# A graph network with routed experts: attention queries in two fp32r parts, expert lists cleared on SyncE's queue

## The chip, the cores and the metric

The kernel runs on one core of one Trainium2 chip. The core has five engines that run side by side, each with its own instruction stream: TensorE (PE, matrix products into PSUM; its weight loads are shown apart as PEld), VectorE (DVE), ScalarE (ACT), GpSimd (POOL) and SyncE (SP). SyncE, ScalarE and GpSimd also issue transfers between SBUF and the device's memory, which 16 DMA engines carry out; "SPq" and "ACTq" in a profile are the issuing instructions on SyncE and ScalarE. Engines wait for each other through semaphores.

The metric is the device time of one execution in microseconds (us). Before the change it is 3965.03 us, the median of three runs (3961.12, 3965.03, 3967.85).

## The reference, cut to what matters

`x` is 3125 nodes by 256 features, with a graph of 53,125 edges (`src`, `dst`, sorted by `dst`). Four pairs of layers follow; each adds to `x`, and each starts with a layer normalization:

```python
x = x + _L0_gnn_ref(_layernorm(x), edge_attr_8, Wq, Wk, Wv, Wo, src, dst)  # attention over the edges, 8 heads
x = x + _L0_ffn_ref(...)   # shared MLP and 4 small experts, the top 2 by a gate
x = x + _L1_gnn_ref(...)   # three rounds of mean aggregation over the edges
x = x + _L1_ffn_ref(...)   # 8 large experts, each node goes to its top 2
x = x + _L2_gnn_ref(...); x = x + _L2_ffn_ref(...)
x = x + _L3_gnn_ref(...); x = x + _L3_ffn_ref(...)
```

The attention:

```python
q = (nfeat @ Wq.T).reshape(n, HEADS, HEAD_DIM) / SCALING
k = (nfeat @ Wk.T).reshape(n, HEADS, HEAD_DIM)
v = (nfeat @ Wv.T).reshape(n, HEADS, HEAD_DIM)
attn = jnp.einsum('ehd,ehd->eh', k[src], q[dst]) + attn_bias
m = jax.ops.segment_max(attn, dst, num_segments=n)
a = jnp.exp(attn - m[dst])
a = a / jax.ops.segment_sum(a, dst, num_segments=n)[dst]
out = jax.ops.segment_sum(v[src] * a[:, :, None], dst, num_segments=n)
return out.reshape(n, FEAT) @ Wo.T
```

## The kernel before, in words

The 3125 nodes are 25 tiles (T) of 125 rows (P), kept in SBUF as `x` for the whole kernel.

**Attention** (`attention`, from L1529). Keys and values of all nodes are written to `kv_d` in the device's memory. Then one loop over the 25 tiles of destination nodes. A tile has a window of 18 chunks (WC) of 128 edges, in three groups of 6 (PC). For a tile:

- `one_hot` makes a one-hot matrix `oh` of each chunk's 128 edges against the tile's 125 rows (bf16), on VectorE.
- `one_hot_turned` transposes it chunk by chunk on TensorE (L1721); ScalarE copies it to `oht` (L1722), 125 by 18 by 128, bf16.
- `queries` multiplies the normalized rows with `Wq`. ScalarE scales the result to `q` (L1710). `q` is then cut into three bf16 parts whose sum is the fp32 value: VectorE rounds the first (L1711) and subtracts it (L1712), ScalarE rounds the second (L1713), VectorE subtracts again for the third (L1714). They lie in `q_t`.
- `logits` has GpSimd gather each edge's key and value row (L1559, one indirect transfer per chunk into a `kv` buffer for 6 chunks; 7 such buffers). For each chunk TensorE multiplies `oht` with the three parts of `q_t`, adding up in PSUM (L1735, 54 products a tile, each with its own weight load); that brings each edge the query of its destination. VectorE multiplies with the keys (L1738) and reduces by head (L1739).
- `sums_of` adds the edges' bias (L1745), takes a first exp (L1748) and sums it per destination with `oh` (L1751, L1753).
- `weights_of` turns the exponent of that sum into a shift `m` (L1759, bf16), brings it to the edges with `oht` (L1763, 18 products of 8 columns), subtracts (L1764), and takes the final exp (L1768).
- `weighted` multiplies values by weights (L1773) and adds them up per destination with an fp32 copy of `oh` (L1778, L1780, `acc`). When `acc` has read a `kv` buffer, GpSimd may gather into it again.
- `normed`, `normed_turned`, `projected` divide, transpose and multiply with `Wo`, and add to `x` (L1804).

The loop is staggered: tile t's logits run beside the weights and sums of tile t-1 and the one-hots and queries of tile t+1.

**Blocks** (`blocks`, from L1855) turn the edge lists into two dense tables of edge counts, `at_d` and `an_d`, that the later convolutions read. For each of 25 steps t: one-hots on VectorE, products (L1954, L1956) into `ab`, a store of `ab` to `at_d`, 25 transposes (L1966) into `an`, a store of `an` to `an_d`. Both stores are on SyncE's queue, each as two transfers (`move`, L105 and L106). `ab` and `an` have two buffers each. The steps are generated one by one between the products of `experts0`, the first experts' layer, so both share the engines.

**Convolutions** (`convolutions`, from L2074) make three passes over `an_d` (`block_pass`, products L2055). Per pass there are seven groups of tiles, and `post` finishes each.

**Expert lists.** For the 8 large experts each node's row is scattered into `xs_d`, a list of 26,880 rows of 260 floats (27.96 MB). Rows that no node fills must be zero, so the list is cleared first. `clear_slots` (L246) is a generator: it makes a tile `nothing` of zeros, 128 by 260, and at each step issues one transfer on ScalarE's queue for one expert (L252, 3380 KB in packets of 1040 B), and a last small one for the spare block (L258). `convolutions` creates it (L2103) and asks for a step at the end of each `post` of the first two passes (L2141). The transfers are collected in `xs_fill`. The router's scatters (L1000, about 2174 to 2373 us) wait for all of them.

Nothing in the code writes the order out by hand: the framework that builds the kernel plans each engine's order by estimated times and due dependencies. A call that is made later in the code can stand earlier on its engine. The profile shows where things came to lie.

Of the kernel before, what the change touches and what calls it, by code (L numbers as in the profile page):

```python
# [68 lines left out]
def gnn_ffn_kernel(ctx: ExitStack, tc: tile.TileContext, a, out: bass.AP):  # L69
# [175 lines left out]

    def clear_slots(pool):  # L246

        nothing = pool.tile([128, DX], F32, name="nothing", bufs=1)
        nc.vector.memset(nothing, 0.0)
        xs_fill.clear()  # L250
        for e in range(8):
            xs_fill.append(nc.scalar.dma_start(  # L252
                xs_d[e * EB * BLK:(e + 1) * EB * BLK, :].rearrange("(p r) d -> p (r d)", p=128)
                .rearrange("p (h d) -> p h d", d=DX),
                nothing.unsqueeze(1).to_broadcast([128, EB * BLK // 128, DX])))
            yield

        xs_fill.append(nc.scalar.dma_start(  # L258
            xs_d[8 * EB * BLK:, :].rearrange("(p r) d -> p r d", p=128),
            nothing.unsqueeze(1).to_broadcast([128, BLK // 128, DX])))  # L260

# [1267 lines left out]
    def attention():  # L1529
# [10 lines left out]
        with ExitStack() as es:  # L1540
# [144 lines left out]

            pool = tiles
            psum = es.enter_context(tc.tile_pool(name="ps_att", bufs=3, space=PSUM, reuse_waits="tile"))

# [15 lines left out]
            def queries(s):  # L1704

                ps = psum.tile([P, D], F32, name="sm")
                product(ps, [(s.lt[:, k, :], wq[:, k, :]) for k in range(2)])
                s.q = pool.tile([P, 3, D], BF16, name="q_t")
                q = pool.tile([P, D], F32, name="q")
                nc.scalar.activation(q, ps, AF.Copy, scale=float(HD) ** 0.5)  # L1710
                nc.vector.tensor_copy(s.q[:, 0, :], q)  # L1711
                nc.vector.tensor_sub(q, q, s.q[:, 0, :])  # L1712
                nc.scalar.copy(s.q[:, 1, :], q)  # L1713
                nc.vector.tensor_sub(s.q[:, 2, :], q, s.q[:, 1, :])  # L1714

            def one_hot_turned(s):
                s.oht = pool.tile([P, WC, 128], BF16, name="oht")
                for c0 in range(0, WC, PC):
# [7 lines left out]
            def logits(s, p):  # L1726
# [4 lines left out]
                for c0 in range(0, PC, 2):  # L1731
                    ps = psum.tile([128, 2, D], F32, name="qx")
                    for c in range(2):
                        for k in range(3):
                            nc.tensor.matmul(ps[:, c, :], s.oht[:, p * PC + c0 + c, :], s.q[:, k, :],  # L1735
                                             start=(k == 0), stop=(k == 2))
                    k_ = kv[:, c0:c0 + 2, KO:VO]
                    nc.vector.tensor_mul(k_, k_, ps)  # L1738
# [16 lines left out]
            def weights_of(s):  # L1755

                m = pool.tile([P, H], BF16, name="m")
                c = 8.0 * math.log(2.0)
# [96 lines left out]
    def blocks(pool, psum):  # L1855
# [84 lines left out]
        ps_n = psum.tile([P, T], F32, name="bdeg", bufs=1)  # L1940

        def hot(name, v, t, n):
            o = pool.tile([128, GT, n], BF16, name=name)
            one_hots(o, v[:, t * GT:(t + 1) * GT, :], iota_h)
            return o

        for t in range(T):
# [14 lines left out]
            for s0 in range(0, T, 8):  # L1962
                n = min(8, T - s0)
                ps = psum.tile([128, 1024], BF16, name="bk")
                for s in range(s0, s0 + n):
# [3 lines left out]
                         ps.rearrange("p (s r) -> p s r", s=8)[:P, :n, :P])  # L1969
            move(nc.sync, an_d[:, t, :], an)  # L1970
            yield
# [21 lines left out]
    def halves(hp, v):  # L1993


        nc.scalar.copy(hp[:, 0], v)  # L1996
        nc.vector.tensor_sub(hp[:, 1], v, hp[:, 0].bitcast(F32))
# [76 lines left out]
    def convolutions(big, bpool):  # L2074
# [7 lines left out]
        with ExitStack() as es:  # L2082
# [19 lines left out]
            pool, route, behind, late = cpool, [], [], []  # L2102
            clear = clear_slots(big)  # L2103

# [5 lines left out]
            for l, bias in enumerate((b0, b1, b2)):  # L2110
                def post(t0, n, agg, l=l, bias=bias):
# [28 lines left out]
                    if l < 2:  # L2140
                        next(clear, None)  # L2141
                        return
# [180 lines left out]
```

## Time and profile before

| | |
|---|---|
| median of three runs | 3965.03 us |
| the profiled execution | 3998.39 us, span 3996.5 us |
| granted TensorE clock, mean | 0.872 |
| busy: PE, PEld, DVE, ACT, POOL | 86%, 64%, 43%, 26%, 15% of the span |
| L1735, 1350 products | 262.0 us busy |
| L1559, 450 gathers | 438.6 us busy, 476.0 us idle before them |
| L252, 8 clears on ScalarE's queue | median 12.05 us each, 1469.8 to 1553.4 us; L258 12.60 us |

How to read it. Times in a row count from the start of the span. "out<-in" names the tile that is written and those that are read; a number in brackets at a row's end is how long the engine was idle before, and what ended that. "issue" means that the profile shows nothing that it waited for. "remote" means that a semaphore moved and the profile does not tell by whom. The granted clock is the share of TensorE's full clock in a stretch; a product at 0.5 takes twice as long. The stages that matter here: attention until about 1060 us, the blocks beside `experts0` until 1447, the rest of `experts0` until 1587, the convolutions from there.

### The profile page before, as it was taken

The page shows a single profiled execution, that of the slowest core. Times are in us where ns is not written, and L with a number is a line of the kernel's source. Part 1 is how long each engine was busy: PE and PEld are TensorE (multiplying, and loading weights), DVE is VectorE, ACT ScalarE, POOL GpSimd, SP SyncE. Part 2 cuts the span into 40 slices and gives each one's busy share as a digit, 9 for nine tenths or more (in the row PEclk, how much of TensorE's full clock was granted, in tenths as well). Part 3 has the DMA queues.
Part 4 walks back from the last instruction along what each step waited for, and adds up shares of the span by engine and source line. Part 5 has one row for each costly group of instructions (what it writes and reads, how often), then busy time and mean ns, then how long its engine had stood idle before and what let it go on. Part 6 is the DMA issues. An engine that isn't in the chain of part 4 may idle for free.

```text
span 3996.5 us, 45148 instructions
## 1 busy us (share of the span) xinstructions
PE 3427.4 (86%) x16645; PEld 2542.0 (64%) x16645; DVE 1728.9 (43%) x4687; ACT 1032.2 (26%) x1931; POOL 609.2 (15%) x588
## 2 busy tenths in 40 slices
PE   6466676676689985999999969997999999999998
PEld 2344555555457652788887848886885555568765
DVE  5355555555667742423235551112562111154562
ACT  1111111211224320333232322222443232332120
POOL 1445444544200000000000132221000000000000
PEclk9677777777767885999999869998989999999898
DMA  6445445444223458334343435665530000024101
GB/s 171 146 135 149 126 124 146 140 129 125 73 80 121 132 162 211 82 97 108 95 110 75 105 115 163 181 185 147 131 88 17 8 16 8 14 63 104 39 1 33
DMA packets 283611, 415.30 MB, mean 104 GB/s; under 512 B 40844, under 2 KB 233137, under 8 KB 283377
## 3 DMA queue, kind: packets, MB, share of 16 engines
q1 hardware_dynamic: 191122, 233.61, 21.1%
q0 software_dynamic: 51568, 134.33, 12.4%
q10 hardware_dynamic: 40687, 44.34, 4.3%
q8 instruction: 135, 2.21, 0.2%
q14 instruction: 99, 0.81, 0.1%
HBM read 313.72 MB, written 98.40 MB: 103 GB/s over the span
## 4 chain that ended last, share of the span: by engine, by line
PE 63%; DVE 2%; ACTq 2%; DMA 1%; ACT 1%; issue 1%; POOL 0%; SPq 0%; DVEq 0%; POOLq 0%
PE po L233 19%; PE agg L2055 18%; PE hid_ps L233 13%; PE tr L233 3%; ACTq L252 1%; PE row L233 1%; PE po L231 1%; PE tok L1439 1%; PE bk L1966 1%; PE tr L223 1%; PE bk L1954 1%; PE tr L2130 1%; DMA x_d<-ys,to 1%; PE bdeg L1956 1%; PE pair L233 0%
## 5 line engine op out<-in xcount | busy, mean ns | idle before, releaser
L2055 PE MATMUL agg<-cnt_f,hp 125*128 125x500 f32 (+1 forms) x3500 | 740.1, 372 | 23.7 <-ACT hp L1996 23.7
L2055 PEld LDWEIGHTS agg<-cnt_f,hp 125*128 125x128 f32 x3500 | 643.9, 191 | 108.6 <-ACT hp L1996 25.0
L1559 POOL DMA_INDIRECT kv<-kv_d,src_w x450 | 438.6, 975 | 476.0 <-PE acc L1780 319.0
L1735 PE MATMUL qx<-q_t,oht 125*128 125x256 bf16 x1350 | 262.0, 355 | 154.2 <-issue 88.7
L2033 ACT CAST cnt_f<-blk 125x500 fp32r<-125x500 bf16 (+1 forms) x435 | 245.9, 566 | 485.5 <-PE agg L2055 468.9
L2033 DVE CAST cnt_f<-blk 125x500 fp32r<-125x500 bf16 (+1 forms) x440 | 185.3, 423 | 295.3 <-PE agg L2055 250.2
L1735 PEld LDWEIGHTS <-oht 125*128 125x128 bf16 x1350 | 164.6, 124 | 230.0 <-issue 180.8
L1286 DVE SCALAR_TENSOR_TENSOR x<-po,gall,x 125x256 f32<-125x256 f32 x200 | 93.8, 483 | 416.2 <-PE po L233 415.7
L1280 ACT ACTIVATE h<-hid_ps,shift,scale 128x500 f32<-128x500 f32 (+1 forms) x224 | 161.9, 723 | 375.9 <-PE hid_ps L233 375.4
L1780 PE MATMUL acc<-kv,oh_f 128*125 128x265 f32 x900 | 212.3, 396 | 21.5 <-DVE kv L1773 21.5
L1738 DVE TENSOR_TENSOR kv<-kv,qx 128x512 f32<-128x512 f32 x225 | 147.3, 682 | 149.5 <-remote 104.6
L1780 PEld LDWEIGHTS acc<-kv,oh_f 128*125 128x125 f32 x900 | 170.1, 191 | 60.8 <-DVE kv L1773 29.0
L233 PE MATMUL hid_ps<-xe,wslot 128*128 128x256 f32 x832 | 194.8, 387 | 10.7 <-DVE xe L1125 10.5
L233 PE MATMUL po<-wslot,h 128*125 128x256 f32 x800 | 203.0, 386 | 0.1
L233 PE MATMUL hid_ps<-h,wslot 128*128 128x500 f32 (+1 forms) x448 | 193.2, 554 | 4.1 <-ACT h L1280 0.6
L233 PEld LDWEIGHTS po<-wslot,h 128*125 128x125 f32 x800 | 145.0, 187 | 75.2 <-ACT h L1280 27.2
L1000 POOL DMA_INDIRECT xs_d<-r_l,pos x50 | 59.5, 1190 | 871.3 <-DVE r_l L996 740.8
L233 PE MATMUL hid_ps<-v_rows,wslot 128*128 128x500 f32 (+1 forms) x448 | 187.2, 538 | 0.0
L233 PE MATMUL po<-wslot,hid 128*128 128x256 f32 x832 | 183.8, 379 | 0.0
L233 PEld LDWEIGHTS hid_ps<-xe,wslot 128*128 128x128 f32 x832 | 148.9, 191 | 44.1 <-DVE xe L1125 13.8
L233 PEld LDWEIGHTS po<-wslot,hid 128*128 128x128 f32 x832 | 158.1, 190 | 21.5
L1132 ACT ACTIVATE hid<-hid_ps,wslot 128x256 f32<-128x256 f32 x208 | 97.0, 474 | 279.8 <-PE hid_ps L233 279.8
(480 smaller groups left out, 4755.6 us busy)
## 6 DMA issues: line engine op xcount, KB each, us to landing
wslot<-in_ex_W SPq DMA_DIRECT2D x52, 1024.0 KB
blk<-an_d SPq DMA_DIRECT2D x60, 546.9 KB
xs_d<-nothing ACTq DMA_DIRECT2D x8, 3380.0 KB
blk<-at_d SPq DMA_DIRECT2D x40, 546.9 KB
blk<-an_d SPq DMA_DIRECT2D x45, 410.2 KB
at_d<-ab SPq DMA_DIRECT2D x25, 683.6 KB
an_d<-an SPq DMA_DIRECT2D x25, 683.6 KB
blk<-at_d SPq DMA_DIRECT2D x30, 410.2 KB
```

The costliest lines, as they stand in the source:

```text
L223: nc.tensor.transpose(ps[:, i * P:(i + 1) * P], src[:, i, k * 128:(k + 1) * 128], ident[:P, :P])
L233: nc.tensor.matmul(ps, l, r, start=(bias is None and i == 0), stop=(i == last))
L1000: st = nc.gpsimd.indirect_dma_start(out=xs_d, in_=l2[:, i, :], in_offset=None, out_offset=bass.IndirectOffsetOnAxis(ap=self.pos[s][:, t0 + ...
L1132: nc.scalar.activation(hid[:, m, :], ps[:, :BLK], AF.Gelu, bias=c[:, 4 + m:5 + m])
L1280: nc.scalar.activation(dst[:, m, :c], ps[:, :c], AF.Relu, bias=shift[:, l, col:col + 1], scale=scale[:, l, col:col + 1])
L1286: nc.vector.scalar_tensor_tensor(x[:, t0 + i, :], po, gating.all[:, t0 + i, e:e + 1], x[:, t0 + i, :], ALU.mult, ALU.add)
L1559: nc.gpsimd.indirect_dma_start(out=kv[:, c, KO:], out_offset=None, in_=kv_d, in_offset=bass.IndirectOffsetOnAxis(ap=src_i[:, at + c:at + c ...
L1735: nc.tensor.matmul(ps[:, c, :], s.oht[:, p * PC + c0 + c, :], s.q[:, k, :], start=(k == 0), stop=(k == 2))
L1738: nc.vector.tensor_mul(k_, k_, ps)
L1780: nc.tensor.matmul(s.acc[:, :D + H + 1], of[:, c, :], kv[:, c, AO:VO], start=(p == 0 and c == 0), stop=(p == 2 and c == PC - 1))
L2033: to(f[:, :n, :], part[0][:, :n, m % MB, :])
L2055: nc.tensor.matmul(ps[f][:, :c], hp[:, m, k, f * 128:(f + 1) * 128], got[:, :c], start=(m == 0 and k == 0), stop=(m == T - 1 and k == 1))
```

## The change

Two things are changed.

In the attention, `q` is cut into two fp32r parts in place of three bf16 ones, by `halves`, a function that the convolutions already use: ScalarE rounds the first part, VectorE subtracts. `oht` becomes fp32r to match and gets a pool of its own, `att_o`, that is opened when the pools of the setup are closed. There are two products per chunk in place of three. `m`, which shares `oht` as weights, becomes fp32r too.

The clearing of `xs_d` is cut into ten transfers of 2.80 MB in place of eight and a small one, with packets of 3120 B from a three times wider tile `nothing`. They are issued on SyncE's queue instead of ScalarE's, in `blocks` after the stores of every second step from t=4 on. Each waits for an earlier `an` store (`stored[-3]`, that of two steps before). The convolutions issue none any more.

```diff
-    def clear_slots(pool):
+    def clear_slots(pool, behind=lambda: None):
-        nothing = pool.tile([128, DX], F32, name="nothing", bufs=1)
+        nothing = pool.tile([128, 3 * DX], F32, name="nothing", bufs=1)
         nc.vector.memset(nothing, 0.0)
+        slots = xs_d.rearrange("(p a r) d -> a p (r d)", p=128, a=10).rearrange("a p (h w) -> a p h w", w=3 * DX)
         xs_fill.clear()
-        for e in range(8):
-            xs_fill.append(nc.scalar.dma_start(
...
+        for part in range(10):
+            st, other = nc.sync.dma_start(slots[part], nothing.unsqueeze(1).to_broadcast([128, 7, 3 * DX])), behind()
+            if other is not None:
+                tc.add_manual_dep(st.ins, other.ins.name, data_dep, reason="in turn")
+            xs_fill.append(st)
             yield
-        xs_fill.append(nc.scalar.dma_start(
-            xs_d[8 * EB * BLK:, :].rearrange("(p r) d -> p r d", p=128),
...
+            turned_pool = es.enter_context(tc.tile_pool(name="att_o", bufs=2, reuse_waits="tile"))
...
-                s.q = pool.tile([P, 3, D], BF16, name="q_t")
+                s.q = pool.tile([P, 2, D], F32R, name="q_t")
                 q = pool.tile([P, D], F32, name="q")
                 nc.scalar.activation(q, ps, AF.Copy, scale=float(HD) ** 0.5)
-                nc.vector.tensor_copy(s.q[:, 0, :], q)
-                nc.vector.tensor_sub(q, q, s.q[:, 0, :])
-                nc.scalar.copy(s.q[:, 1, :], q)
-                nc.vector.tensor_sub(s.q[:, 2, :], q, s.q[:, 1, :])
+                halves(s.q, q)
...
-                s.oht = pool.tile([P, WC, 128], BF16, name="oht")
+                s.oht = turned_pool.tile([P, WC, 128], F32R, name="oht")
...
-                        for k in range(3):
+                        for k in range(2):
                             nc.tensor.matmul(ps[:, c, :], s.oht[:, p * PC + c0 + c, :], s.q[:, k, :],
-                                             start=(k == 0), stop=(k == 2))
+                                             start=(k == 0), stop=(k == 1))
...
-                m = pool.tile([P, H], BF16, name="m")
+                m = pool.tile([P, H], F32R, name="m")
...
+        stored = []
+        clear = clear_slots(pool, lambda: stored[-3])
...
-            move(nc.sync, an_d[:, t, :], an)
+            stored.append(move(nc.sync, an_d[:, t, :], an))
+            if t > 2 and t % 2 == 0:
+                next(clear, None)
             yield
...
-            clear = clear_slots(big)
...
                     if l < 2:
-                        next(clear, None)
                         return
```

`halves`, unchanged:

```python
def halves(hp, v):
    nc.scalar.copy(hp[:, 0], v)
    nc.vector.tensor_sub(hp[:, 1], v, hp[:, 0].bitcast(F32))
```

## The prediction

> **What bounds the kernel now.** I read four views, in this order: the page's chain of waits, that chain in order of time, the timeline of the stages that the diff touches, and rows of single tiles. The chain says TensorE almost throughout, with one part that is no engine's work:
>
> ```profile
> PE 63%; DVE 2%; ACTq 2%; DMA 1%; ACT 1%; issue 1%; POOL 0%; SPq 0%; DVEq 0%; POOLq 0%
> ```
>
> In order of time that part lies in one place, the end of the first experts' layer:
>
> ```profile
> 1481.66 9.27 ACTq L252
> 1491.63 11.71 ACTq L252
> ...
> 1516.76 11.86 ACTq L252
> 1528.88 12.31 ACTq L252
> 1541.81 11.51 ACTq L252
> 1554.41 11.71 issue
> ```
>
> These six make 68.4 us. They are the clears of `xs_d`. ScalarE's timeline shows what they do: the code asks for one per group of the convolution, but all nine were placed ahead of it, between the last activations of `experts0`, and the queue holds the engine while its transfers drain:
>
> ```profile
> 1528.67 0.21 ACT L707 ACTIVATE g<-g 125x12 f32<-125x12 f32 x1 [11.91 <-issue]
> 1528.69 12.50 ACTq L252 DMA_DIRECT2D xs_d<-nothing  x1
> 1541.24 0.57 ACT L750 ACTIVATE s<-tr,wslot 128x375 f32<-128x375 f32 x1 [12.36 <-issue]
> ```
>
> The reader sees activations of 0.2 and 0.6 us waiting 12 us each. The stretches (PE, PEld, DVE, ACT, POOL busy; clock; DMA share; GB/s) say the same: from 1470 to 1570 the DMA engines are full (1.08, 280 GB/s) and TensorE works 53 of 100 us, while in the block building before it DMA is at 0.39:
>
> ```profile
> 160.00:1060.00 900.00, 624.05 (x3808) 469.10 (x3807) 505.01 (x805) 166.06 (x321) 399.50 (x409) 0.75 0.43 125
> 1130.00:1450.00 320.00, 292.95 (x2241) 218.34 (x2240) 218.00 (x390) 108.95 (x177) 0.15 (x1) 0.76 0.39 123
> 1470.00:1570.00 100.00, 53.01 (x127) 25.76 (x126) 14.31 (x47) 7.86 (x16) 0.00 (x0) 0.67 1.08 280
> ```
>
> Attention (160 to 1060) is bound by none of these alone. POOL issues a tile's 18 gathers (1.25 us apart, 22.6 us), then waits for `acc` of the tile before to free buffers:
>
> ```profile
> 506.59 0.95 POOL L1559 DMA_INDIRECT kv<-kv_d,src_w  x1 [0.30 <-issue]
> 520.25 0.95 POOL L1559 DMA_INDIRECT kv<-kv_d,src_w  x1 [12.71 <-PE acc L1780]
> ```
>
> The waits between 300 and 900 give 222.3 us in 16 such waits, 13.9 us each. So a tile is 22.6 + 13.9 = 36.5 us. While gathers run, TensorE's results are seen late: ScalarE takes up `q` (L1710) at 498.39 although TensorE's last product for it starts at 492.25, and VectorE waits 6.43 us for TensorE at 506.88. Work saved there is mostly not on the path. What counts is from the last gather to the first third of `acc`: `sums`, `m`, the 18 products L1763, the subtraction L1764, exp, L1773, `acc`.
>
> **Part 1, the clears leave ScalarE's queue.** Removed: nine issues on ACT (1469.84 to 1566.1) and a memset of 0.28 us. I rebuild the tail without them from what the last-but-one group shows. Its gate chain, product L233 into `tr` to transpose L740, took 1463.62 to 1469.59, 6.0 us; the last group's took 1504.37 to 1529.75, 25.4: 19.4 saved. From L740 to `tr<-s` it took 5.6 us (1469.59 to 1475.23) against 12.1 (1529.75 to 1541.87): 6.5 saved. The waits of TensorE on `e` and `s` of L750 later on (4.78 and 7.20) and earlier (2.92), and 7.29 for `lt`, are 22.2, of which I leave 3 for the ordinary hand-overs. That is 45.1. The last stretch, 1567.8 to 1585.2, is 17.4 us at half clock (1570 to 1600: 0.56); at full clock a third to a half less, 6 to 9, and the earlier cold pieces (1504 to 1515) 3 to 5 more. Sum 54 to 59; I take 57. Ends: 45 (idle alone, the clock stays low) and 68.4 (all of the chain's pieces). Nothing later takes it back: the next blocks were fetched from 1451 on, and the convolution's normalization starts with the last addition to `x`.
>
> Added: ten clears on SP's queue in the block building, from t=4 to t=22, every second t. Each is 896 packets of 3120 B, 56 per DMA engine. A 1040 B packet of the old clears moved at 280 GB/s over all engines, so 2.8 MB take 10 us at that rate, and in 24 us (two steps) the added share is at most 10/24 = 0.42 beside 0.39: it fits. It is hidden behind VectorE, ScalarE and TensorE, which build the next `ab` and `an`. SP waits before each clear for the `an` store of two steps earlier, issued some 25 us before. Queued behind the clear on SP are the next stores (an `at_d` store follows `an_d` by 6 to 10 us: 1382.17 to 1388.12, 1405.51 to 1415.39); they would land up to 10 us minus that gap later. `ab` and `an` have two buffers each and a step is 12.3 us ((1446.57-1147.9)/24), so a store may be late by about one step less its own few microseconds before VectorE's evacuation waits. If that cover were gone, each clear would cost up to 3 us, 30 in all; that is the upper end. Lower end: the memset, 780 columns, 0.28 x 3 = 0.8. I take 3, nearer the lower end, because no evacuation in this stage now waits for a store. The scatters of the router wait for ten fills instead of nine, 750 us after the last: nothing. A first issue on ACT took 0.68 us, and ScalarE was held only from the third on, with 6,656 packets already queued; 896 a time on SP do not fill that.
>
> The Trainium skill, "DMA: Bandwidth & Descriptors", section "Issuing engines are not separate DMA queues", says that choosing another issuing engine saves only the sequencer's issue time, which is usually small against the transfer. By that rule alone the move would be worth about zero and the sum would be 3 + 5 = +8 us, 3973; the rows above show issue times of 12 us on an engine that others wait for, and they decide.
>
> **Part 2, two fp32r parts.** Per tile 54 pairs of weight load and product at L1735 become 36, VectorE loses L1711 (0.31) and one of L1712 and L1714 (0.42), ScalarE's copies L1713 and L1722 keep their size. `m` becomes fp32r, and `oht`, the weights of both products, too. The rows for the weight loads (min, median, max in ns):
>
> ```profile
> L1735 PEld LDWEIGHTS <-oht x1350: 95/105/185, 158.7 to 1035.0; 125*128 125x128 bf16 x193
> L1763 PE MATMUL sm<-m,oht x450: 166/168/214, 181.5 to 1041.2; 125*128 125x8 bf16 x150
> ```
>
> ```profile
> L2130 PEld LDWEIGHTS tr<-ident_r,hp x300: 187/192/338, 1674.1 to 2330.7; 125*128 125x128 f32 x150
> ```
>
> and for the pace, from the timeline:
>
> ```profile
> 510.93 0.65 PE L1763 MATMUL sm<-m,oht 125*128 125x8 bf16 x18 [0.88 <-DVE m L1759]
> ...
> 1707.44 1.90 PE L2130 MATMUL tr<-ident_r,hp 125*128 125x126 f32 x16
> ```
>
> L2130 is fp32r on both sides, 128 columns of weights, 126 streamed: (1.90-0.28)/15 = 108 ns a pair. Its load sets that, and a load of 128 fp32r columns is 192-105 = 87 ns dearer than one in bf16. L1763's pairs now run at (0.65-0.17)/17 = 28 ns. With fp32r weights they take 108 at full clock and twice that at half: 18 x 80 = +1.4 us, or 18 x 188 = +3.4. L1735 goes from 54 x 109 ((1.69-0.27)/13, the fourteen at 552.37) = 5.9 us to 36 x 112 = 4.0; at half clock from 11.5 to 7.7. So TensorE gains 0.4 to 0.5 us a tile, but what it loses is on the path and part of what it gains is not. At 510.9 VectorE has 1.9 us of other products before L1764, so of +3.4 (the clock is low there) 0 to 2.1 shows, 1.0 in the middle; in the other tiles (551.9, backlog of L1735 ahead of `m`) the two cancel. Mean +0.3 x 25 = +8, less 3 for the first tile, whose fp32r parts are ready at about 159.5 where L1735 now starts at 163.0. I take +5. Ends: +50 (2.1 in every tile) and -37 (below, and tile 0).
>
> The Trainium skill, "TensorE: Matmul & The Clock Gate", section "Weight-path perf modes — Fast Weight Load (FWL) and DoubleRow", gives fast loads to 128 weights of a type other than FP32, and leaves open where fp32r stands; counted as not FP32, L1763 would cost nothing more and this part would be some -3 us. The rows of L2130 say it is loaded at the slow pace.
>
> **Sum.** -57 + 3 + 5 = -49 us. The profiled execution took 3998.39 us (span 3996.5 and 1.9 around it) and becomes 3949; the median of the runs shown is 33.4 lower, 3965.03, and becomes 3916.
>
> **Rivals.**
> A, attention gains instead. Short waits of POOL are 12.7, the mean is 13.9; if the shorter chain to `q_t` lets every tile take the short one (the long ones hold L1712 and L1714 at 542.48 and 544.48, just ahead of the path), 1.2 x 24 = 29 us go, and the loss on L1763 is covered: 3916 - 8 - 26 = 3882. Against it: in the long tile VectorE then waits for TensorE until 546.14 anyway.
> B, slower than before: fp32r at 256 columns is not one pass. L2130 excludes four passes at 126 columns, not two. At the fp32 pace of 256 columns (216 ns, 32 in 6.91 us) L1735 costs 36 x 216 = 7.8 us for 5.9, at half clock 15.4 for 11.5: +2.9 a tile over part 2, 25 x 2.9 = 72, so 3988. It decides from 49/25 = 2.0 us a tile on. Against it: L2055 streams 500 fp32r columns in 226 ns ((43.73-0.4)/192).
> C, the clears crowd the stores: the 30 above in place of 3, 3943, and if `experts0` waits with them, about 3955.
> D, the change frees ScalarE's queue, but the tail is then held by its gate chain and a cold clock: 20 instead of 57, 3953.
>
> **How the numbers follow.** Chances: forecast 0.62 (own range 3895 to 3940), A 0.18, B 0.07, C 0.08, D 0.05. What a measurement here can tell from no change is about 0.2%, 8 us: faster is below 3957. All of the forecast and A, most of C and D lie there: 0.87; within 0.2%: 0.05 (tails of C and D); slower: 0.08 (B and 0.01 of mishap). The range takes in A, C and D and leaves out B and a tail below A: 3878 to 3958.
>
> **What would show it.** No ACTq L252 on the chain and ScalarE without waits of 12 us after the block building; about 55 us less between the last `an_d` store and the first `agg`. DMA share between 1190 and 1410 about 0.7, with the steps still near 12.3 us. L1763's 18 products near 2 us (half clock: 3.8) instead of 0.65; L1735's pairs at 110 ns. POOL's mean wait for `acc` 13.5 to 15 us. The prediction is wrong if that wait moves by over 2 us either way, or if VectorE in the block building waits for stores.

## The result, and the profile after

The changed kernel takes 3978.32 us (median of 20 runs, 3962.53 to 3988.62), the kernel before 3963.41 us on the same chip (20 runs, 3952.04 to 3981.73). The ratio is 1.0036, with a 95% interval of 1.0024 to 1.0047: slower by 0.36%, some 14 us. The forecast was 3916 us, faster.

The two first profiles hide this: before's execution took 3998.39 us, after's 3962.53. A second profiled execution of each, shown among the experiments, took 3955.62 and 3977.39. So the size of a stage is given below from both pairs.

The change is the sum of two large effects of opposite sign. Times in us from the start of the span, read from the four traces; `agg` (L2055) is the convolutions' product, and its first marks their start:

| | before | before, second | after | after, second |
|---|---|---|---|---|
| end of the last `acc` | 1055.4 | 1040.9 | 1112.3 | 1120.8 |
| from there to the first `agg` | 545.0 | 524.7 | 475.3 | 475.5 |
| from the first `agg` to the end | 2396.2 | 2388.1 | 2373.0 | 2379.1 |
| span | 3996.5 | 3953.7 | 3960.7 | 3975.4 |

Attention became 57 us longer in the first pair and 80 in the second; the stretch with the blocks and `experts0` became 70 and 49 shorter; the rest 23 and 9.

**Blocks and `experts0`.** The chain of waits of the changed kernel, by engine (its page's fourth part), has no part left on ScalarE's queue:

```profile
PE 77%; DVE 7%; another core or an unknown queue 5%; issue 4%; DMA 3%; ACT 2%; POOL 1%; SPq 0%; ACTq 0%; DVEq 0%; POOLq 0%
```

The other shares can't be compared with those of before: the chain of before, followed back from the end, stops at 1189.4 us and leaves attention out, while this one reaches back to the start. What it has on VectorE, "another core or an unknown queue" and "issue" comes for the most part from attention. The stretches of the changed kernel (PE, PEld, DVE, ACT, POOL busy; clock; DMA share; GB/s), the blocks and then the 100 us that were the tail before:

```profile
1181.00:1569.00 388.00, 346.38 (x2430) 243.46 (x2429) 240.86 (x500) 115.59 (x195) 0.15 (x1) 0.80 0.50 172
1470.00:1570.00 100.00, 83.58 (x549) 55.50 (x549) 61.23 (x155) 28.83 (x52) 0.15 (x1) 0.81 0.49 172
```

From 1470 to 1570 TensorE now works 84 us where it worked 53, and DMA is half full where it was full. The reader also sees something that was not forecast: the blocks last 388 us, not 303. A step takes 16.0 us from store to store where it took 12.4, because the planner has spread the 25 steps over nearly the whole of `experts0`: between the first and the last transpose of the blocks TensorE has 518 products of L233, the helper with which `experts0` multiplies, where it had 313. After the last `an_d` store only 17.6 us are left to the first `agg` (1570.0 to 1587.6), against 153.7 before (1446.6 to 1600.3). SyncE's timeline shows two of the clears, each behind the `an` stores of its step, with 13.4 us to the next store:

```profile
1301.61 0.30 SPq L105 DMA_DIRECT2D an_d<-an  x1
1301.96 0.40 SPq L106 DMA_DIRECT2D an_d<-an  x1
1302.40 1.24 SPq L253 DMA_DIRECT2D xs_d<-nothing  x1
1315.76 0.30 SPq L105 DMA_DIRECT2D at_d<-ab  x1
...
1333.92 1.27 SPq L253 DMA_DIRECT2D xs_d<-nothing  x1
```

**Attention.** Lines have moved by three to five: the gathers are L1556, the logits' products L1730, `m`'s products L1758, `acc` L1775. The groups of instructions (busy, mean ns of one | idle before):

```profile
L1775 PE MATMUL acc<-kv,oh_f 128*125 128x265 f32 x900 | 230.0, 419 | 13.0 <-DVE kv L1768 12.3
L1730 PE MATMUL qx<-q_t,oht 125*128 125x256 f32 x900 | 222.1, 414 | 105.6 <-DVE kv L1733 65.7 <-issue 29.7 <-ACT q L1708 5.6
...
L1758 PE MATMUL sm<-m,oht 125*128 125x8 f32 x450 | 97.0, 348 | 90.5 <-DVE m L1754 90.5
```

In the same view of before, `acc` and `m` are

```profile
L1780 PE MATMUL acc<-kv,oh_f 128*125 128x265 f32 x900 | 212.3, 396 | 21.5 <-DVE kv L1773 21.5
L1763 PE MATMUL sm<-m,oht 125*128 125x8 bf16 x450 | 16.2, 169 | 12.1 <-DVE m L1759 12.1
```

`m`'s products grew from 16.2 to 97.0 us busy. `acc`, which the change does not touch, became 17.7 us dearer. Who pays for `m` stands in VectorE's waits during attention, after

```profile
DVE l L1759 <- PE sm L1758: 60.7, 25, 3.8
```

and before:

```profile
DVE l L1764 <- PE sm L1763: 0.5, 2, 0.3
```

25 waits, one in each tile, 2.4 us each. The timeline of one odd tile of the changed kernel gives the place:

```profile
528.22 3.97 PE L1758 MATMUL sm<-m,oht 125*128 125x8 f32 x18 [7.62 <-DVE m L1754]
...
532.23 0.30 DVE L1759 TENSOR_TENSOR l<-l,sm 128x144 f32<-128x144 f32 x1 [2.34 <-PE sm L1758]
...
534.86 5.09 DVE L1768 TENSOR_TENSOR kv<-kv 128x1536 f32<-128x1536 f32 x3
...
536.66 8.31 PE L1775 MATMUL acc<-kv,oh_f 128*125 128x265 f32 x36 [0.47 <-DVE kv L1768]
...
539.88 0.95 POOL L1556 DMA_INDIRECT kv<-kv_d,src_w  x1 [15.23 <-PE acc L1775]
```

From `m`'s first product to the multiplication by the weights is 6.64 us; before it was 4.3 (510.9 to 515.2). The granted clock in attention fell: 0.75 between 300 and 900 us before, 0.69 after.

```profile
300.00:900.00 600.00, 414.64 (x2525) 311.04 (x2524) 328.87 (x525) 112.55 (x216) 291.89 (x299) 0.75 0.47 136
300.00:900.00 600.00, 424.17 (x2122) 368.11 (x2120) 308.76 (x472) 103.44 (x203) 273.15 (x277) 0.69 0.43 126
```

POOL's wait for `acc` between 300 and 900 is now 15.97 us on average (255.5 in 16), 2.07 more than in the first trace of before; the prediction called itself wrong from 2 on.

```profile
POOL kv L1556 <- PE acc L1775: 255.5, 16, 17.1
```

I cut that wait, from the end of a tile's last gather to the next tile's first, into four pieces (means of tiles 3 to 20, from the starts and ends in the traces):

| us a tile | before | before, second | after | after, second |
|---|---|---|---|---|
| last gather to first product of `m` | 5.14 | 4.70 | 4.09 | 4.16 |
| from there to the multiplication by weights | 3.76 | 3.75 | 6.07 | 6.08 |
| to the first product of `acc` | 1.81 | 1.81 | 1.80 | 1.81 |
| to the next gather (a third of `acc`) | 3.22 | 3.23 | 3.97 | 4.22 |
| sum | 13.93 | 13.49 | 15.94 | 16.27 |

`m` starts 0.5 to 1.0 earlier, its products cost 2.3 more, `acc`'s first third 0.75 to 1.0 more. 25 tiles times 2.0 to 2.8 are 50 to 70 us.

### The profile page after: what moved, and what is told of

The parts are those of the page before. It is cut to its first block, busy times and chain, and to the rows that moved or that the text cites. A ratio compares the mean times of both kernels' runs of the same rounds, so it can differ in the third digit from the quotient of the medians.

```text
span 3960.7 us, 44186 instructions
## 1 busy us (share of the span) xinstructions
PE 3422.2 (86%) x16195; PEld 2627.6 (66%) x16195; DVE 1710.9 (43%) x4637; ACT 1026.0 (26%) x1929; POOL 613.3 (15%) x588
## 3 DMA queue, kind: packets, MB, share of 16 engines
q0 software_dynamic: 51568, 134.33, 12.3%
## 4 chain that ended last, share of the span: by engine, by line
PE 77%; DVE 7%; another core or an unknown queue 5%; issue 4%; DMA 3%; ACT 2%; POOL 1%; SPq 0%; ACTq 0%; DVEq 0%; POOLq 0%
PE po L233 19%; PE agg L2055 18%; PE hid_ps L233 13%; PE acc L1775 5%; PE tr L233 3%; PE sm L1758 2%; PE qx L1730 2%; PE sm L233 1%; PE row L233 1%; PE bk L1964 1%; DVE kv L1768 1%; PE po L231 1%; PE tok L1436 1%; PE bdeg L1954 1%
## 5 line engine op out<-in xcount | busy, mean ns | idle before, releaser
L2055 PE MATMUL agg<-cnt_f,hp 125*128 125x500 f32 (+1 forms) x3500 | 734.4, 370 | 24.4 <-ACT hp L1996 24.4
L2055 PEld LDWEIGHTS agg<-cnt_f,hp 125*128 125x128 f32 x3500 | 638.8, 190 | 108.7 <-ACT hp L1996 25.8
L1556 POOL DMA_INDIRECT kv<-kv_d,src_w x450 | 441.0, 980 | 524.8 <-PE acc L1775 336.7
L1730 PE MATMUL qx<-q_t,oht 125*128 125x256 f32 x900 | 222.1, 414 | 105.6 <-DVE kv L1733 65.7
L1730 PEld LDWEIGHTS qx<-q_t,oht 125*128 125x128 f32 x900 | 188.7, 303 | 122.6 <-DVE kv L1733 78.0
L1775 PE MATMUL acc<-kv,oh_f 128*125 128x265 f32 x900 | 230.0, 419 | 13.0 <-DVE kv L1768 12.3
L1775 PEld LDWEIGHTS acc<-kv,oh_f 128*125 128x125 f32 x900 | 182.4, 206 | 56.8 <-DVE kv L1768 19.7
L233 PE MATMUL hid_ps<-xe,wslot 128*128 128x256 f32 x832 | 194.8, 387 | 11.0 <-DVE xe L1122 10.9
L233 PE MATMUL po<-wslot,h 128*125 128x256 f32 x800 | 203.0, 386 | 0.1
L233 PE MATMUL hid_ps<-h,wslot 128*128 128x500 f32 (+1 forms) x448 | 192.5, 552 | 4.1 <-ACT h L1277 0.6
L233 PEld LDWEIGHTS po<-wslot,h 128*125 128x125 f32 x800 | 145.0, 187 | 75.2 <-ACT h L1277 27.2
L233 PE MATMUL hid_ps<-v_rows,wslot 128*128 128x500 f32 (+1 forms) x448 | 187.2, 538 | 0.0
L233 PE MATMUL po<-wslot,hid 128*128 128x256 f32 x832 | 183.8, 379 | 0.0
L233 PEld LDWEIGHTS hid_ps<-xe,wslot 128*128 128x128 f32 x832 | 149.0, 191 | 44.4 <-DVE xe L1122 14.1
L1758 PE MATMUL sm<-m,oht 125*128 125x8 f32 x450 | 97.0, 348 | 90.5 <-DVE m L1754 90.5
L233 PEld LDWEIGHTS po<-wslot,hid 128*128 128x128 f32 x832 | 158.1, 190 | 21.5
```

Of the source, the lines that this page charges most:

```text
L233: nc.tensor.matmul(ps, l, r, start=(bias is None and i == 0), stop=(i == last))
L1556: nc.gpsimd.indirect_dma_start(out=kv[:, c, KO:], out_offset=None, in_=kv_d, in_offset=bass.IndirectOffsetOnAxis(ap=src_i[:, at + c:at + c ...
L1758: nc.tensor.matmul(ps[:, c, :], s.oht[:, c, :], m, start=True, stop=True)
L1775: nc.tensor.matmul(s.acc[:, :D + H + 1], of[:, c, :], kv[:, c, AO:VO], start=(p == 0 and c == 0), stop=(p == 2 and c == PC - 1))
L2055: nc.tensor.matmul(ps[f][:, :c], hp[:, m, k, f * 128:(f + 1) * 128], got[:, :c], start=(m == 0 and k == 0), stop=(m == T - 1 and k == 1))
```

## Experiments

Theory M: the change is two effects; the 18 products that bring `m` to the edges, now with fp32r weights, cost 2.3 us in every tile. The rivals are C (the clears bring little), Q (the logits' own fp32r products are at fault) and, after the first four experiments, K (TensorE's clock follows its load, so less work can cost time). These letters are not those of the prediction's rivals. Kernels are compared with the kernel before on the same chip, by ratio, since its median there lay between 3962 and 3974 us; "us" below is (ratio - 1) x 3963.

### Each part alone

`e1_clears_only` keeps the change's `clear_slots`, its calls in `blocks` and their removal from `convolutions`, and takes back the attention:

```diff
-                s.q = pool.tile([P, 2, D], F32R, name="q_t")
+                s.q = pool.tile([P, 3, D], BF16, name="q_t")
...
-                s.oht = turned_pool.tile([P, WC, 128], F32R, name="oht")
+                s.oht = pool.tile([P, WC, 128], BF16, name="oht")
...
-                m = pool.tile([P, H], F32R, name="m")
+                m = pool.tile([P, H], BF16, name="m")
```

> The clears on SyncE's queue as in the change, the attention as before. Theory M (the change is two opposite effects: the moved clears save, and the 18 slow products for m cost 2.3 us in each of 25 tiles, +58 us): since the whole change is +15, this kernel is 15 - 58 = -43 us against the kernel before, about 3920, with attention's last acc at about 1044 us as before and no issue of 12 us on ScalarE. Rival C (the moved clears bring little, because something later takes the time back, and the attention costs only about as much as the whole): 3950 to 3965.

`e2_fp32r_only` is the reverse: that attention part on the kernel before.

> Two fp32r parts of q, fp32r oht and m as in the change; the clears stay on ScalarE's queue. Theory M: +58 us, about 4021; acc's last burst at about 1102 us; the tail with its six 12 us issues stays. Rival C: +15 to +25, about 3980 to 3990, and the attention's later end is partly caught up in the blocks.

Measured: clears alone 3921.64 us, ratio 0.9865 (0.9845 to 0.9884), -53 us. Attention alone 4035.24 us, ratio 1.0153 (1.0132 to 1.0174), +61 us. The sum, +8, stands beside +14 for the whole. M's figures, -43 and +58, are met within 10; C is out.

### Which product

`e3_m_bf16`, from the whole change: a second copy of `oht`, in bf16, is the weights of `m`'s products alone.

```diff
                 s.oht = turned_pool.tile([P, WC, 128], F32R, name="oht")
+                s.oht_h = turned_pool.tile([P, WC, 128], BF16, name="oht_h")
...
+                    nc.scalar.copy(s.oht_h[:, c0:c0 + PC, :].rearrange("d c e -> d (c e)"),
+                                   ps[:P, :PC * 128])
...
-                m = pool.tile([P, H], F32R, name="m")
+                m = pool.tile([P, H], BF16, name="m")
...
-                    nc.tensor.matmul(ps[:, c, :], s.oht[:, c, :], m, start=True, stop=True)
+                    nc.tensor.matmul(ps[:, c, :], s.oht_h[:, c, :], m, start=True, stop=True)
```

> The whole change, but m stays bf16 and ScalarE writes a second, bf16 copy of oht (3 copies of 0.8 us a tile more) that is the weights of the 18 products for m; the two fp32r products for the logits stay. Theory M: these 18 products are back at 0.65 us, and the 2.3 us a tile go: 58 us below the whole change, about 3920. Rival Q (the path was lengthened by the fp32r products of the logits, at 213 ns a pair and a lower clock, and m's slow loads are hidden): as the whole change, 3970 to 3985. In between, if the 2.4 us of copies a tile hold ScalarE ahead of the exp.

`e4_m_fp32r`, from the kernel before: the same in the other direction, an fp32r copy `oht_r` and an fp32r `m`, the logits left in bf16.

```diff
+                s.oht_r = turned_pool.tile([P, WC, 128], F32R, name="oht_r")
...
-                m = pool.tile([P, H], BF16, name="m")
+                m = pool.tile([P, H], F32R, name="m")
...
-                    nc.tensor.matmul(ps[:, c, :], s.oht[:, c, :], m, start=True, stop=True)
+                    nc.tensor.matmul(ps[:, c, :], s.oht_r[:, c, :], m, start=True, stop=True)
```

> The kernel before with only m and the weights of its 18 products made fp32r (a second copy of oht in fp32r, 3 copies of 0.8 us a tile more on ScalarE); the three bf16 parts of q and the clears as before. Theory M: +2.3 us a tile, 58 us, about 4021. Rival Q: no more than the 8 us that I had in the prediction, 3965 to 3975.

Measured: `e3` 3929.26 us, ratio 0.9888 (0.9871 to 0.9906), -44 us; against the whole change 59 us gained, M's 58. That the two figures meet is in part luck: in the traces the last `acc` comes 39 and 48 us earlier than in the two of the changed kernel and the wait is 1.3 to 1.6 us a tile shorter, not 2.3, since `acc` became dearer (below). `e4` 4076.61 us, ratio 1.0259 (1.0238 to 1.0280), +103 us. Q is out on both sides. `e4` is a miss in size: its wait is 4.24 us a tile longer than before's, of which 2.8 lie between `m` and the multiplication by weights, 1.2 ahead of `m`, 0.3 behind. That the 1.2 come from ScalarE's three added copies was not tried by itself; in `e3`, with the same copies, `m` is not late.

But `e3` should have kept something of the two products for three, and by ratio it is 0.2% behind `e1`. The groups of `e3` say where:

```profile
L1778 PE MATMUL acc<-kv,oh_f 128*125 128x265 f32 x900 | 248.9, 444 | 17.7 <-DVE kv L1771 17.7
...
L1761 PE MATMUL sm<-m,oht_h 125*128 125x8 bf16 x450 | 16.2, 169 | 65.1 <-DVE m L1757 65.1
```

`m` is back at 16.2 us, as before the change; `acc` is at 444 ns a product, 396 before. In all of tiles 3 to 20 the granted clock was 0.5 when `acc` began, in the kernel before in one of them. Theory K reads it so: TensorE's work ahead of `acc` had become so light that the clock was still down.

### Less work or more

If that is right, useless work should help. `e5_third_zero` is `e3` with a third product per chunk whose right side is zero:

```diff
-                        for k in range(2):
+                        for k in range(3):
                             nc.tensor.matmul(ps[:, c, :], s.oht[:, p * PC + c0 + c, :],
-                                             s.q[:, k, :],
-                                             start=(k == 0), stop=(k == 1))
+                                             s.q[:, k, :] if k < 2 else zero_r,
+                                             start=(k == 0), stop=(k == 2))
```

> As the kernel with the whole change and m on a bf16 copy of oht, and a third fp32r product per chunk whose right side is zero: 18 more products a tile that add nothing to the result. In that kernel the first 12 products of acc took 4.62 us a tile, all of them started at a clock of 0.5, against 2.79 in the kernel before. Theory K (the granted clock follows TensorE's load: with fewer products it is still at 0.5 when acc starts): the added work lifts the clock before acc, its first 12 products fall to about 2.8, and attention is not longer, up to 1.8 us a tile shorter, 3885 to 3930 in all. Rival W (more work is only more work): 18 x 0.21 = 3.9 us a tile more, half of it on the path: 50 us longer than that kernel's 3929, about 3980.

`e6_two_bf16` asks the same from the other side: `e1` with the third bf16 part of `q` left out.

```diff
-                s.q = pool.tile([P, 3, D], BF16, name="q_t")
+                s.q = pool.tile([P, 2, D], BF16, name="q_t")
...
-                nc.vector.tensor_sub(s.q[:, 2, :], q, s.q[:, 1, :])
...
-                        for k in range(3):
+                        for k in range(2):
```

> The clears moved as in the change; the attention as before, but q in two bf16 parts, the third left out (a less exact q): 18 products and one subtraction less a tile, and m's fast loads kept. It asks what fewer products are worth at all. Theory K: m comes earlier by 1 to 2 us a tile, but acc's first products fall to the low clock and give 1 to 1.8 back: 3905 to 3930, about the 3922 of the kernel with the clears alone. Rival A of the prediction (a shorter chain to q_t lets every tile take the short wait): 26 to 29 us below that kernel, about 3894.

Measured: `e5` 3898.30 us, ratio 0.9815 (0.9796 to 0.9835), -73 us, 29 below `e3` for 450 products more that add nothing. `e6` 3940.40 us, ratio 0.9914 (0.9898 to 0.9930), -34 us: 19 slower than `e1` for 450 products and 25 subtractions less, and 10 above the upper end that K had been given, so the clock gave back more than the products saved. The timelines of one tile each, `e3` and then `e5`, show the same 36 products of `acc`:

```profile
519.92 10.20 PE L1778 MATMUL acc<-kv,oh_f 128*125 128x265 f32 x36 [0.45 <-DVE kv L1771]
```

```profile
507.71 8.30 PE L1784 MATMUL acc<-kv,oh_f 128*125 128x265 f32 x36 [0.68 <-DVE kv L1777]
```

and their stretches from 300 to 900, `e3` and then `e5`:

```profile
300.00:900.00 600.00, 402.72 (x2176) 334.99 (x2175) 317.74 (x480) 138.21 (x256) 283.18 (x288) 0.68 0.45 132
```

```profile
300.00:900.00 600.00, 412.82 (x2562) 363.15 (x2560) 321.26 (x499) 146.40 (x267) 297.42 (x303) 0.76 0.47 139
```

386 products more, 10 us more of TensorE's time, and the clock is at 0.76 for 0.68; 15 more of POOL's instructions fit into the same 600 us. In the cut of POOL's wait, `acc`'s first third falls from 5.06 to 3.20 us a tile, `m` comes 0.9 later, the piece between `m` and the weights is 0.6 shorter: 14.65 to 13.12. `e6` shows the other direction: `acc`'s first third takes 4.57 us a tile, in the odd tiles 5.22, where `e1` has 3.22.

A second pair of this kind leaves the chain that makes `q_t` as short as `e6`'s and gives the products back. `e12_two_bf16_third_zero` is `e6` with a zero third product; its `q` stays in two bf16 parts.

```diff
-                        for k in range(2):
+                        for k in range(3):
...
-                            nc.tensor.matmul(ps[:, c, :], s.oht[:, p * PC + c0 + c, :], s.q[:, k, :],
-                                             start=(k == 0), stop=(k == 1))
+                            nc.tensor.matmul(ps[:, c, :], s.oht[:, p * PC + c0 + c, :],
+                                             s.q[:, k, :] if k < 2 else zero_h,
+                                             start=(k == 0), stop=(k == 2))
```

> The kernel with the clears alone and q in two bf16 parts, and a third bf16 product per chunk whose right side is zero, so that TensorE has the 54 products a tile of the kernel before; only the third part of q, and the subtraction that makes it, is left out. Theory K: the clock before acc is back, so the 19 us that two parts lost against the clears alone (3940 to 3922) go: 3915 to 3925. Theory A' (besides, the shorter chain from q to q_t is what let the even tiles take the short wait in the fp32r kernel with the zero product, 3898): below that, 3895 to 3908.

Measured: 3903.58 us, ratio 0.9847 (0.9817 to 0.9877), -61 us, 27 below `e6`; `acc`'s first third is back at 3.21 us a tile, and that 1.36 us is the whole difference between the two waits (14.68 and 13.35). The microseconds lie in the range of A', but the kernel before ran 10 us faster beside `e12` than beside `e6`, and by ratio `e12` is level with `e1` within both intervals. Whether the shorter chain adds a few microseconds stays open.

`e11_after_third_zero` puts the zero product on the whole change, with `m` left on fp32r weights.

```diff
-                        for k in range(2):
+                        for k in range(3):
...
+                                             s.q[:, k, :] if k < 2 else zero_r,
```

> The whole change with a third fp32r product per chunk whose right side is zero; m stays on the fp32r weights. With this the four cases of slow or fast m and two or three fp32r products are complete: fast and two 3929, fast and three 3898, slow and two 3978. Theory M and K together: acc's first products are at full clock again (0.75 us a tile less), m's slow loads stay (2.3 us a tile), and the third product puts m later by up to 1 us: 3950 to 3985. If the added work also lifts the clock before m, its 18 products take 2.0 us for 3.9 and it ends near 3935. Rival W (more work is only more work): above 4000.

Measured: 3970.86 us, ratio 1.0018 (1.0001 to 1.0035), +7 us. With it the table is complete (us against the kernel before):

| | two fp32r products | and a zero third |
|---|---|---|
| `m` on fp32r weights | +14 (the change) | +7 |
| `m` on a bf16 copy | -44 | -73 |

`m`'s weights are worth 59 and 80 us, the clock 7 and 29. In `e11` `acc`'s first third is at 3.21 us, as theory K asks, but `m` comes 0.9 us later than in the changed kernel and `acc` starts 0.5 later behind the weights, so the sum of the wait, 16.42, is not better than the change's 15.94 and 16.27. The 18 products of `m` stayed slow: 3.65 us a tile.

### Queue or place

Part 1 moved the clears twice: to another queue, and to another place. `e7_act_in_blocks` is `e1` on ScalarE's queue; `e8_sp_old_place` is the kernel before with the clears where they were, on SyncE's.

```diff
-            st, other = nc.sync.dma_start(slots[part], nothing.unsqueeze(1).to_broadcast([128, 7, 3 * DX])), behind()
+            st, other = nc.scalar.dma_start(slots[part], nothing.unsqueeze(1).to_broadcast([128, 7, 3 * DX])), behind()
```

> The kernel with the clears alone, with its ten clears in the same place beside the blocks, but issued on ScalarE's queue in place of SyncE's. Theory S (the gain comes from ScalarE no longer being held when nine transfers of 3.4 MB are issued back to back; one of 2.8 MB in 25 us doesn't fill the queue): within 10 us of the clears alone, 3920 to 3932. Rival E (it is ScalarE's part in issuing that costs, anywhere): each issue holds ScalarE some 5 to 10 us among the evacuations of the blocks, and of the 53 us gained half or more goes: 3945 to 3975.

```diff
-            xs_fill.append(nc.scalar.dma_start(
+            xs_fill.append(nc.sync.dma_start(
```

> The kernel before with its nine clears unchanged in size and place in the code, but issued on SyncE's queue. Theory S (the cost is the issuing engine being held): most of the gain, 40 to 55 us below the kernel before, unless the fetches of the first convolution pass stand behind the clears on SyncE's queue. Rival O (the DMA engines, full for 100 us at the end of experts0, are what counts, so the clears must lie beside the blocks): at the kernel before, within 10 us.

Measured: `e8` 3918.77 us, ratio 0.9856 (0.9833 to 0.9879), -57 us, all that `e1` brings. Its SyncE timeline shows the queue held as ScalarE's was, seven clears in a row between two fetches of the first convolution pass (the last two come at 1606.9, among later fetches):

```profile
1473.23 0.47 SPq L106 DMA_DIRECT2D blk<-an_d  x1
1473.74 68.74 SPq L252 DMA_DIRECT2D xs_d<-nothing  x7
1565.42 0.32 SPq L105 DMA_DIRECT2D blk<-an_d  x1
```

The fetch at 1565.42 came 22.9 us after the last of the seven, so the clears' issue did not hold it up, and the first `agg` had begun at 1534.1 on blocks fetched earlier. From 1470 to 1570, the tail of before, the DMA engines are nearly as full as they were there (0.96 for 1.08), and yet TensorE works 90 us where it worked 53:

```profile
1470.00:1570.00 100.00, 89.90 (x353) 56.25 (x352) 56.11 (x191) 29.64 (x70) 0.00 (x0) 0.93 0.96 258
```

So full DMA engines cost little here, and a held ScalarE nearly all of the 57 us. O is out; in the changed kernel the place beside the blocks was not needed for the gain.

`e7` 3947.09 us, ratio 0.9926 (0.9908 to 0.9944), -29 us. Some 24 of `e1`'s 53 us are lost. The number lies at the near end of E's range, but not by E's mechanism: each issue took 0.38 us, so ScalarE was not held,

```profile
L253 ACTq DMA_DIRECT2D xs_d<-nothing x10: 378/379/423, 1189.5 to 1426.1; - x10
```

and its waits for stores add up to 6.9 us. The trace has the last `acc` to first `agg` at 495.5 us (`e1` 485.7) and the three passes of the convolutions together at 703.0 (`e1` 689.8). The planner laid both out in another order than in `e1`, with the tail of `experts0` behind the blocks again, so the order may cost the 24 us. But `e8` has that tail too, and there the blocks take 297 us from the first transpose to the last, in `e7` 315 for as many products (313 and 311 of L233). In `e7` the ten steps that hold a clear take 15.5 us on average, the other fourteen 11.2; the ten also hold more products (101 and 81 a step). Whether the order or the clears' traffic beside the steps (DMA share 0.62 for 0.40 in `e8`) costs the time, no run separates.

By the Trainium skill, "DMA: Bandwidth & Descriptors", section "Issuing engines are not separate DMA queues", starting transfers from several engines saves only the time that starting them takes, usually small beside the transfer. Here that time was 12 us for most of the clears, on SyncE as on ScalarE; `e8` moves it from the one to the other and gains 57 us, since others waited for ScalarE and nobody for SyncE.

### The same kernels again

> The kernel before, unchanged: a second profiled execution. The first took 3998.39 us, some 25 to 35 us above the medians of this kernel. If that came by chance, this one takes 3955 to 3985 and shows which stage was longer in the first; if a profiled execution is longer wherever the nine clears are issued back to back, it is again 3985 to 4000 and the surplus lies between 1447 and 1600 us.

> The kernel with the whole change, unchanged: a second profiled execution. The first took 3962.53, the lowest of its 20. Expected 3970 to 3985, with attention's last acc some 10 to 20 us later than the 1112 of the first: which tiles take acc at the low clock differs from run to run.

Measured: 3955.62 and 3977.39 us. The second columns of the two tables above are these. The first execution of before was longer in attention (14 us), in the stretch with the clears (20) and in the rest (8); the second execution has none of it, so it came by chance. The attention of after differs by 8.5 between its two.

## Why the prediction was wrong

**Part 1 was right in its sum, in part by luck.** -57 and +3 were forecast; the clears alone measure -53 us, within the ends. Two of the steps behind it did not happen as told. The block steps were to stay near 12.3 us with DMA at about 0.7: they take 16.0 us with DMA at 0.50, since the planner spread them over `experts0`. The tail that I rebuilt piece by piece does not exist in the changed kernel; in `e8`, where it does, from the last `an_d` store (1442.6) to the first `agg` (1534.1) it takes 91.4 us against 153.7 and, in the second execution of before, 143.6 (1422.0 to 1565.6): 52 to 62 saved, close to the 57. There the last group's gate chain, rebuilt at 6.0 us, takes 6.1 (1489.48 to 1495.58). So the mechanism holds for `e8`; that the changed kernel, in another order, gains as much was not foreseen. Evacuations wait for a store once, 3.6 us, so "no evacuation waits" was nearly right. `e8` also shows that the move beside the blocks, which I priced, was not what paid.

**Part 2 was wrong, and it decided.** +5 was forecast, +61 measured alone, beyond the upper end of +50. The prices of the instructions were right: `m`'s products take 3.8 to 3.97 us for 0.65, as told for the low clock, and L1730's pairs run at 114 to 120 ns at full clock and 213 at half. What failed is the step from price to path: "of +3.4 [...] 0 to 2.1 shows, 1.0 in the middle; in the other tiles [...] the two cancel. Mean +0.3 x 25 = +8". In the runs 2.3 show in every tile, odd and even: of the 3.2 to 3.3 added, only 0.9 to 1.0 stayed behind VectorE's other work. In the even tiles, between the first product of `m` and the multiplication by weights, the median went from 3.21 to 5.50, in the odd ones from 4.30 to 6.63. In the odd tiles the prediction's own row gave the upper figure, 2.1, and halving it had no reason behind it; nothing offsets the 2.3 there, as `m` starts no earlier (3.5 us after the last gather before and after). In the even tiles `m` starts 2.1 us earlier in the first pair of traces and 1.1 in the second, so the two nearly cancel in one and by half in the other. Net of that the slow products cost 1.3 to 1.8 us a tile, 32 to 45 in all, where the prediction had 0.3 and 8. The 3 us credited to the first tile did not come: the first `acc` starts at 186.7 and 188.6, before at 186.7 and 181.8.

**The clock was taken as given.** I priced fewer products at full and at half clock, and did not ask whether fewer products change the clock. They do: `acc`'s first third, on the path, became 0.75 to 1.0 us a tile dearer, 19 to 25 in all, so the part of part 2 that should have gained gives its gain back. This term was not in the sum at all; `e5` and `e6` show it with both signs, and `e12` gives back what `e6` lost.

**What the readings missed.** The first view, read as "TensorE almost throughout", stops at 1189.4 us and says nothing of attention, where the time was lost. Some of the arithmetic is a little off, and none of it decides: 1.0 in every second tile is a mean of 0.5, not 0.3; (1446.57-1147.9)/24 is 12.4, not 12.3; A's 29 us enter its sum as 26; and the second issue on ScalarE already took 3.84 us, where the text has it held only from the third on.

**The rivals.** B (fp32r at 256 columns in two passes) is refuted by L1730's pairs of 213 ns at half clock, as fast as the bf16 products were there. A (every tile takes the short wait) did not come about in the change, but `e5` comes near it: the median wait of its even and odd tiles is 12.85 and 12.73, and three even tiles wait 14.0 to 16.2. C and D, on the clears, are refuted by `e1`. The kernel came out on the slower side by a mechanism that the prediction priced, as the end of a range, and held for unlikely.

**The signs named in advance** did their work in part. No clear is on the chain, and the products of `m` take near 3.8 us. The steps of 12.3 us, the DMA share of 0.7 and the 55 us less between the last `an_d` store and the first `agg` (136 less, as the tail is gone) did not come. POOL's wait moved by over 2 us, which was called the sign of a wrong prediction, and it was.

## What to carry to other kernels

When a type changes, count every product that shares the operand: the logits gained a third of their products, but 18 short products with the same weights lost their fast loads, and they stood where nothing covered them. A stall that one engine suffers while it issues transfers can be cured by another queue alone; look for the engine that nobody waits for, before looking for a better place. And TensorE's clock belongs into the sum: work taken away just ahead of a critical burst can make the burst slower, so that the fastest kernel here, 3898.30 us (ratio 0.9815), is the one with 450 products by zero in it.

## What was not expected of the hardware

- Pairs of weight load and product of 8 columns took 213 ns (median) with fp32r weights at a granted clock of 0.5, and 27 ns with bf16 weights at the same clock (112 and 25 at 1.0; the 112 from `e11`). The fp32r pairs of 256 columns on the same weights took 213 as well: with 8 columns the load alone sets the pace. The Trainium skill, "TensorE: Matmul & The Clock Gate", section "Weight-path perf modes — Fast Weight Load (FWL) and DoubleRow", promises fast loads of 128 weights to types other than FP32; in these runs fp32r does not get them.
- The granted clock changed between 0.5 and 1.0 some 50 times in attention, and every distance between two changes is a multiple of 3.41 us. So a microsecond less of work ahead of `acc` moves the rise by a whole step or not at all. The same page, section "What's actually happening", tells of free-running windows of about 3.4 us, a busy one of which lifts the clock and an idle one lowers it; the grid of the traces agrees with such windows.
- Where a burst of `acc` starts in the low half, its 36 products take 10.20 us for 8.30.
